# Column halves in the even steps, side sums one by one, and a round's next weights on VectorE: a change to a three-level fast matrix product in fp32

## The chip, the core and the metric

The kernel runs on one core of one Trainium2 chip. A core has a matrix engine (TensorE, PE in the profile; its weight loads are shown as PEld), three engines for elementwise work (VectorE or DVE, ScalarE or ACT, GpSimd or POOL) and SyncE (SP), whose queue here only issues transfers between the chip's main memory and the core's on-chip memory (SBUF). PE writes its results to eight accumulator banks (PSUM), each 128 partitions by 512 fp32 columns. Each engine works through its own list of instructions in order; an instruction that waits holds back everything behind it on its engine.

The metric is the device time of one launch in microseconds (us). Lower is better.

## What is computed

`x` has 32 batches of 128 channels by 2048 positions, all fp32. Cut to what matters here:

```
def reference(x, cond, ...):
    # a 128x128 mixing matrix per batch, made from cond by a small network and a softmax
    y = einsum('boi,bih->boh', agg_w, x) + agg_b
    # a 2048x2048 matrix W plus 16 low-rank updates, applied along the positions
    x = x + einsum('bsd,od->bso', y, W) + bias + low_rank(y)
    # a grouped convolution of 9 taps, then a blockwise MLP over permuted channels
    z = conv(x) + ctx + b
    return x + unpermute(down(gelu(up(permute(z)))))
```

The kernel multiplies `x` by the updated `W` first (the mixing matrix acts on the other axis and follows later). That product, 4096 rows by 2048 by 2048, is what the change is about.

## The kernel before

**The product.** It is a Strassen-Winograd scheme in three levels. At each level a 2x2 block product is made of seven products P1 to P7 of sums of blocks instead of eight.

- *Outer level:* seven rounds, in the order `P1, P2, P6, P7, P5, P3, P4` (`ROUNDS`). A round uses one sum of blocks of `W` as weights, and runs eight steps, `g` = 0 to 7, one for each group of four batches (512 columns of `x` transposed). `x_loads` fetches the blocks of `x` for a step, `x_combine` makes their sum `a` (in place, by `pieces`, line 282) and its four inner sums `s` (lines 310 to 313), all on GpSimd. Partial results (`p`, `u`, `c`) are fetched for a step by `part_load`, added to, and stored by `part_store`.
- *Inner level:* the round's weights need four sums per 128-row chunk: `inner_weights` makes `t1`, `t2`, `t4` (lines 251 to 253) and a difference in place (line 255). These are 16 GpSimd instructions of 128x512 for each round. They are issued in step 7 of the round ahead (in step 6 for the second round). The raw weights of the next round come from main memory through `outer_weights`, in steps 2 to 6.
- *Third level:* the rounds in `THIRD` (P2, P6, P7, P5, P3) take their steps in pairs. A step makes some of the seven inner products whole, each of four 128x512 matmuls: P1, P6, P7 in the four "wide" rounds, and P1, P5, P6, P3, P7 in round P5. The others (P2 and P4, in wide rounds also P3 and P5) are made for both steps of the pair together, in the odd step, again by seven products each: `quarter(w, k, ...)`, four matmuls of 128x256 that fill one bank (line 495). Their weight sums are made by `third_weights` in step 0: by GpSimd in `apart` (line 398), and by VectorE from a list `quarter_ops`, two at a time at the `between(j)` points of step 0 (line 1177), eight in a wide round, four in round P5. Their sums of `x` are made on VectorE by `first_inputs` (at the end of the even step) and `second_inputs` (in the odd step, behind the first addition): four instructions each in `third_inputs`, lines 431 to 434.

**The order around the change** is written out by hand. In `multiply_third` a product is four matmuls into a bank `px` (line 479), and VectorE adds the bank to the result in SBUF at once (`add`, line 469; `add_two` for P7, line 473). The next product goes on accumulating in the same bank, so its first matmul waits until VectorE has read the bank:

```
        product("P1", px, True, False)
        add(0, 0, px)
        ...
        product("P6", px, False, False)
        add(0, 1, px)
```

In an even step nothing stands between the two; in an odd step quarters do, in other banks. The quarters' results are added by lines 505 and 508.

**Between rounds P1 and P2** a side chain (`small()`, a generator that is advanced once or twice a step) makes the mixing matrices: `mixed_kernels` multiplies, copies each bank with ScalarE into one of three small buffers (line 610), and sends it out by four transfers of 32x512 from ScalarE's own queue (line 614). ScalarE also copies banks to the results in round P1 (line 344).

**Buffers.** Nearly everything lies in 24 rotating buffers of 128x2048 (`slot`); a new tile waits until the one that had its buffer has been read for the last time. SP's queue issues all loads and result stores in program order.

Of the kernel before, what the change touches and what calls it, by code (L numbers as in the profile page):

```python
# [11 lines left out]
ALU = mybir.AluOpType  # L12
# [4 lines left out]
P = 128  # L17
B = 32
# [37 lines left out]
def adaln_ffn_kernel(  # L56
# [184 lines left out]
        for ki in range(2):  # L241
            nc.vector.tensor_tensor(wsum[:, oh], wsum[:, oh], t[:, ki], ALU.add)

    def inner_weights(name, ts, between=lambda kc: None):

        t1, t2, t4 = (slot(f"{name}_t{k}", (P, 4, QW)) for k in (1, 2, 4))
        tt = nc.gpsimd.tensor_tensor
        for kc, t in enumerate(ts):
            between(kc)
            b11, b12, b21, b22 = (t[:, ki, oi] for ki in range(2) for oi in range(2))  # L250
            tt(t1[:, kc], b12, b11, ALU.subtract)
            tt(t2[:, kc], b22, t1[:, kc], ALU.subtract)
            tt(t4[:, kc], b21, t2[:, kc], ALU.subtract)
        for t in ts:
            tt(t[:, 0, 1], t[:, 1, 1], t[:, 0, 1], ALU.subtract)
        return {
            "t4": t4,
            "P1": [t[:, 0, 0] for t in ts], "P2": [t[:, 1, 0] for t in ts],
            "P3": [t[:, 1, 1] for t in ts], "P7": [t[:, 0, 1] for t in ts],
            "t1": t1, "P4": [t4[:, kc] for kc in range(4)], "P5": [t1[:, kc] for kc in range(4)],  # L260
            "P6": [t2[:, kc] for kc in range(4)],
        }
# [32 lines left out]
    def x_combine(r, g, ts):  # L295

        a = ts[0]
        tt = nc.gpsimd.tensor_tensor
# [8 lines left out]
        xa[steps.index((r, g))] = a  # L307
        s = slot(f"s_{r}{g}", (P, 4, QW))
        a11, a12, a21, a22 = a[:, 0, 0], a[:, 1, 0], a[:, 0, 1], a[:, 1, 1]
        tt(s[:, 1], a21, a22, ALU.add)  # L310
        tt(s[:, 2], s[:, 1], a11, ALU.subtract)
        tt(s[:, 3], a11, a21, ALU.subtract)
        tt(s[:, 0], a12, s[:, 2], ALU.subtract)
        xs_[steps.index((r, g))] = s
# [5 lines left out]
    xa, xs_ = {}, {}  # L320


    ADDED = {
        "P1": [(None, "p1")],
# [55 lines left out]
    def third_weights(name, rhs):  # L380
# [12 lines left out]
        def apart(k, t):  # L393

            for kc in range(2):
                (r11, r12), (r21, r22) = (halves(rhs[k][2 * h + kc]) for h in range(2))
                for op in sums(r11, r12, r21, r22, [v and v[:, kc] for v in t]):
                    nc.gpsimd.tensor_tensor(*op, ALU.subtract)

        def together(n, t):  # L400
            (r11, r12), (r21, r22) = (
# [25 lines left out]
    def third_inputs(x, t):  # L427

        (x11, x12), (x21, x22) = x
        tt = nc.vector.tensor_tensor  # L430
        tt(t[0], x21, x22, ALU.add)
        tt(t[1], t[0], x11, ALU.subtract)
        tt(t[3], x12, t[1], ALU.subtract)
        tt(x21, x11, x21, ALU.subtract)
        return {
            "P1": x11, "P2": x12, "P3": t[3], "P4": x22,
            "P5": t[0], "P6": t[1], "P7": x21,
        }
# [7 lines left out]
    def first_inputs(i):  # L446

        a, b = xa[i], xa[i + 1]
        return third_inputs(
            [blocks_of(t[:, 1]) for t in (a, b)],  # L450
            [as_two(a[:, 0, 1]), as_two(b[:, 0, 1]), None, as_two(a[:, 0, 0])],
        )

    def second_inputs(i):
        a, b = xs_[i], xs_[i + 1]
        return third_inputs(
            [blocks_of(t[:, 0:2]) for t in (a, b)],
            [as_two(a[:, 2]), as_two(a[:, 3]), None, as_two(xa[i + 1][:, 0, 0])],
        )

    def multiply_third(i, r, g, lhs, olds, between, rhs, quarters, sq):
# [2 lines left out]
        py = None if wide else bank()  # L464
        both = [held.pop(), olds] if sq else []

        def add(si, oi, ps):
            for acc in olds:
                nc.vector.tensor_tensor(acc[:, si, oi], ps, acc[:, si, oi], ALU.add)  # L469

        def add_two(ps):
            for acc in olds:
                nc.vector.tensor_tensor(
                    acc[:, 1], ps.unsqueeze(1).to_broadcast([P, 2, QW]), acc[:, 1], ALU.add
                )

        def product(k, ps, first, last):
            for kc in range(4):
                nc.tensor.matmul(  # L479
                    ps, lhsT=lhs[k][:, bass.ts(kc, P)], rhs=rhs[k][kc],  # L480
                    start=first and kc == 0, stop=last and kc == 3, skip_group_check=True,
                )

        qs = [{n: bank() for n in "xyz"} for w in quarters if sq and w is not None]
        xq = [sq]
# [1 line left out]
        def quarter(w, k, *to):  # L487
# [24 lines left out]
        product("P1", px, True, False)  # L512
        add(0, 0, px)
        if sq and wide:
            xq.append(second_inputs(i - 1))
        between(0)
        for w in range(2 if sq else 0):
            quarter(w, "P1", (0, 0))
            quarter(w, "P2", (0, 0))
        if not wide:  # L520
            product("P5", py, True, False)
            add(1, 1, py)
        between(1)
        if not wide and sq:
            quarter(0, "P6", (0, 1))
            quarter(0, "P5", (1, 1))
        product("P6", px, False, False)
        add(0, 1, px)
        between(2)
        if wide:  # L530
            for w in range(2 if sq else 0):
                quarter(w, "P6", (0, 1))
                quarter(w, "P5", (1, 1))
        elif sq:
            quarter(0, "P7", (1, 1))
            quarter(0, "P3", (0, 1))
        if not wide:
            product("P3", py, False, True)
            add(0, 1, py)
            done(py)  # L540
            between(3)
            if sq:
                quarter(0, "P4", (1, 0))
        product("P7", px, False, True)
        add_two(px)
        done(px)
        if wide:
            between(3)
            for k, to in (("P7", (1, 1)), ("P3", (0, 1)), ("P4", (1, 0))):
                for w in range(2 if sq else 0):  # L550
                    quarter(w, k, to)
        between(4)
        between(5)
        if not sq:
            held.append(olds)
            return
        for b, accs in enumerate(both):
            for (_, new), acc in zip(ADDED[r], accs):
                part_store(new, g - 1 + b, acc, nc.sync)
# [35 lines left out]
    def mixed_kernels(j, bd):  # L595

        w = mix.rearrange("p i o -> p (i o)")
        rows_of = [slice(h * P // 2, (h + 1) * P // 2) for h in range(2)]
        for n in range(2):
            cols = slice(n * QW, (n + 1) * QW)  # L600
            ps = [bank() for h in range(2)]
            for h in range(2):
                m = 2 * h + j
                nc.tensor.matmul(
                    ps[h], lhsT=bd[rows_of[h], m * P : (m + 1) * P], rhs=w[rows_of[h], cols],
                    start=True, stop=True,
                )
            for h in range(2):
                t = conv_tile(0, 4 * j + 2 * n + h, ("cq", "cs", "cr")[(2 * n + h) % 3])
                nc.scalar.copy(t, ps[h])  # L610
                done(ps[h])
                for q in range(4):
                    o0 = (4 * (2 * h + j) + q) * 2 * QW + n * QW
                    nc.scalar.dma_start(ag_d[:, o0 : o0 + QW], t[q * B : (q + 1) * B])

    def mix_loads(b):
        g, tp, s = b // GB, b % GB // 2, b % 2
# [306 lines left out]
    def small():  # L924
# [80 lines left out]
            nc.vector.tensor_scalar(orow[:, g], pos, g * L, None, ALU.add)  # L1005
        yield
        for j in range(2):
            mixed_kernels(j, bd)
            yield

        while len(made) < 16:
            yield
# [104 lines left out]
    for i, (r, g) in enumerate(steps):  # L1117
        ri = i // NG
        last_round = ri + 1 == len(ROUNDS)
        if i + 1 < len(steps):  # L1120
            if i + 1 not in xs:
                xs[i + 1] = x_loads(*steps[i + 1])
            if not last_round:
                lhs[i + 1] = x_combine(*steps[i + 1], xs.pop(i + 1))
                if r in THIRD and g == 0:
                    quarters, quarter_ops = third_weights(r, rhs)
        if i == 0:
            olds_load(0)
        if i + 1 < len(steps) and not last_round:
# [2 lines left out]
        if ahead and steps[i + 2][0] != "P6":  # L1132
            xs[i + 2] = x_loads(*steps[i + 2])
        if g == NG - (1 if ri else 2) and ri < len(ROUNDS) - 1:
            nxt = inner_weights(ROUNDS[ri + 1], [nxt[kc] for kc in range(4)])

        if ri == 0:
            ks = blocks[4 + 2 * g : 6 + 2 * g]
# [20 lines left out]
                waiting[g - 2] = outer_weights(ROUNDS[ri + 1], g - 2)  # L1159

        if last_round and g == 0:
            late_loads()
        if last_round and g == 2:

# [6 lines left out]
        def between(j):  # L1171
            if ri == 0 and j == 2:
                for k in blocks[6 + 2 * g : 8 + 2 * g]:
                    wt[k] = w_load(*k)
            for _ in range(2):
                if r in THIRD and j < 4 and quarter_ops:
                    nc.vector.tensor_tensor(*quarter_ops.pop(0), ALU.subtract)
# [124 lines left out]
```

## Time and profile before

| | |
|---|---|
| Time, median of 3 runs | 2681.66 us (2679.14 to 2686.1) |
| The profiled execution | 2681.12 us, its span 2679.4 us |
| PE busy | 2581.2 us, 96% of the span |
| DVE, POOL, ACT busy | 1544.7 us (58%), 1336.3 us (50%), 537.5 us (20%) |
| Granted PE clock | 0.99 over the span |
| Matmul, 128x512 at line 479 | 1088 records, two for each matmul |
| Result additions, lines 469 and 505, 128x512 from a bank | 683 to 689 ns |
| POOL at line 282 (`pieces`) | 1390 ns mean, 128 of `xt<-xt,xt` |

How to read it: one fp32 matmul leaves two PE records. PE records overlap (the mean of one 128x512 record is 592 ns or more, but one starts every 429 ns when nothing is waited for), so what a matmul costs is read from the distance between starts. "Idle before" is the time in which the engine had nothing to run before the instruction, with the instruction of another engine that ended the wait. A tile name such as `P_t` stands for all of a kind, here the inner sums `t1`, `t2`, `t4`; `wo_P` are raw weights of a round, `P_q` quarters' weight sums, `p` and `u` partial results.

### The profile page before, as it was taken

To read this page: it belongs to the slowest core of one execution; us is meant where nothing else is said; L and a number is where in the kernel's file an instruction comes from. 1 tells how busy PE (TensorE), PEld (TensorE's weight loads), DVE (VectorE), ACT (ScalarE), POOL (GpSimd) and SP (SyncE) were. 2 spreads that over 40 slices of the span, in tenths; PEclk is the share of its full clock that TensorE was granted. 3 is DMA by queue.
4 is the path that set the end of the run, shared out by engine and by line. 5 is a ranking of instruction groups with operands and counts; after the bars stand their busy time and mean duration, and the time that the engine had idled before them with its cause. 6 is when DMAs were issued, how large, how long until landed. Compare 5 with 4: busy or idle time off the path is not lost. (4 is left out here: it accounts for less than half of the span.)

```text
span 2679.4 us, 22365 instructions
## 1 busy us (share of the span) xinstructions
PE 2581.2 (96%) x7350; PEld 1394.7 (52%) x7350; DVE 1544.7 (58%) x2326; ACT 537.5 (20%) x1107; POOL 1336.3 (50%) x1086
## 2 busy tenths in 40 slices
PE   9999799989889999999999999999999999999998
PEld 4444366656556655466544555445555445555543
DVE  4554166655466566665446766666666666666600
ACT  0000100000000000000001234444444444444432
POOL 7221466897786674687423324444333444443322
PEclk9999899999999999999999999999999999999999
DMA  7542357758646476755567688777877777877532
GB/s 313 204 173 110 96 229 257 301 218 323 229 187 283 189 284 267 301 218 216 200 223 247 223 289 278 246 227 245 253 239 224 226 229 241 250 231 232 164 132 86
DMA packets 185091, 608.40 MB, mean 227 GB/s; under 512 B 17680, under 2 KB 88848, under 8 KB 140944
## 3 DMA queue, kind: packets, MB, share of 16 engines
q1 hardware_dynamic: 149936, 473.74, 49.9%
q0 software_dynamic: 32704, 130.04, 14.4%
q10 hardware_dynamic: 2336, 3.19, 0.4%
q8 instruction: 59, 0.97, 0.1%
q14 instruction: 56, 0.46, 0.1%
HBM read 372.51 MB, written 200.84 MB: 214 GB/s over the span
## 5 line engine op out<-in xcount | busy, mean ns | idle before, releaser
L884 PE MATMUL bank<-t,ws 128*128 128x512 f32 x1024 | 460.3, 592 | 0.0
L895 PE MATMUL bank<-gl,ws 128*128 128x512 f32 x1024 | 460.2, 592 | 0.0
L902 POOL DMA_INDIRECT out<-t,orow x128 | 152.9, 1194 | 540.9 <-DVE t L900 462.9
L887 ACT ACTIVATE gl<-bank 128x512 f32<-128x512 f32 x512 | 306.2, 598 | 445.3 <-PE bank L884 441.6
L895 PEld LDWEIGHTS bank<-gl,ws 128*128 128x128 f32 x1024 | 194.6, 190 | 233.0 <-issue 230.8
L884 PEld LDWEIGHTS bank<-t,ws 128*128 128x128 f32 x1024 | 194.6, 190 | 226.6 <-issue 222.9
L633 POOL TENSOR_TENSOR x<-x,fb 128x512 f32<-128x512 f32 x128 | 176.4, 1407 | 219.5 <-DMA x<-in_x 189.3
L900 DVE TENSOR_TENSOR t<-bank,t 128x512 f32<-128x512 f32 x128 | 88.4, 691 | 319.2 <-PE bank L895 319.2
L639 ACT ACTIVATE bank<-w,aggb 128x512 f32<-128x512 f32 x128 | 80.8, 683 | 899.6 <-DMA w<-w_d 882.1
L282 POOL TENSOR_TENSOR xt<-xt,xt 128x512 f32<-128x512 f32 x128 | 173.5, 1390 | 120.6 <-DMA xt<-in_xT 67.0
L310 POOL TENSOR_TENSOR s_P<-xt 128x512 f32<-128x512 f32 x56 | 75.1, 1341 | 295.9 <-DMA xt<-in_xT 218.6
L479 PE MATMUL bank<-P_t,s_P 128*128 128x512 f32 x384 | 178.1, 609 | 33.0 <-DVE p L469 24.3
L479 PE MATMUL bank<-wo_P,s_P 128*128 128x512 f32 x320 | 149.4, 613 | 18.9 <-DVE u L469 13.2
L868 POOL DMA_INDIRECT t<-hx_d,row x128 | 131.4, 1026 | 50.4 <-issue 25.3
L505 DVE TENSOR_TENSOR u<-bank,u 128x512 f32<-128x512 f32 x168 | 111.6, 687 | 63.4 <-PE bank L495 61.7
L479 PEld LDWEIGHTS bank<-P_t,s_P 128*128 128x128 f32 x384 | 73.0, 194 | 123.7 <-issue 103.8
L349 PE MATMUL bank<-P_t,s_P 128*128 128x512 f32 x256 | 115.3, 604 | 13.3 <-ACT m_P L344 13.3
L740 PE MATMUL bank<-va,tw_l 128*128 128x256 f32 x512 | 121.6, 380 | 0.4 <-DVE va L724 0.4
L495 PE MATMUL bank<-P_q,xt 128*128 128x256 f32 x480 | 112.9, 386 | 8.6 <-DVE u L505 4.6
L740 PEld LDWEIGHTS bank<-va,tw_l 128*128 128x128 f32 x512 | 96.9, 190 | 42.0 <-issue 32.2
L651 DVE TENSOR_TENSOR x<-bank,x 128x512 f32<-128x512 f32 x128 | 87.7, 690 | 49.3 <-POOL x L633 23.9
L648 PE MATMUL bank<-u,agl 128*128 128x512 f32 x256 | 115.1, 592 | 0.0
(207 smaller groups left out, 3971.4 us busy)
## 6 DMA issues: line engine op xcount, KB each, us to landing
xt<-in_xT SPq DMA_DIRECT2D x88, 1024.0 KB, 10.0
u<-u_d SPq DMA_DIRECT2D x40, 1024.0 KB, 10.0
wo_P<-wb_d SPq DMA_DIRECT2D x36, 1024.0 KB, 12.0
u<-c_d SPq DMA_DIRECT2D x64, 512.0 KB, 7.2
x<-in_x SPq DMA_DIRECT2D x32, 1024.0 KB, 7.9
xg<-x SPq DMA_DIRECT2D x256, 128.0 KB, 5.4
hx_d<-x1t SPq DMA_DIRECT2D x32, 1024.0 KB, 6.0
hx_d<-ht SPq DMA_DIRECT2D x32, 1024.0 KB, 7.0
```

Of the source, the lines that this page charges most:

```text
L282: nc.gpsimd.tensor_tensor(out[:, i, j], a[:, i, j], b[:, i, j], op)
L349: nc.tensor.matmul(ps, lhsT=lhs[k][:, bass.ts(kc, P)], rhs=rhs[k][kc], start=first and kc == 0, stop=last and kc == 3, skip_group_check=True,)
L479: nc.tensor.matmul(ps, lhsT=lhs[k][:, bass.ts(kc, P)], rhs=rhs[k][kc], start=first and kc == 0, stop=last and kc == 3, skip_group_check=True,)
L495: nc.tensor.matmul(out, lhsT=xq[w][k][:, i, bass.ts(kc, P)], rhs=quarters[w][i][k][kc], start=k in ("P1", "P2", "P5") and i == 0 and kc == ...
L633: nc.gpsimd.tensor_tensor(xt[:, f], xt[:, f], late["fb"][:, f], ALU.add)
L648: nc.tensor.matmul(pm, lhsT=ag, rhs=u[:, f], start=False, stop=True, skip_group_check=True)
L740: nc.tensor.matmul(out, lhsT=w[:, 2 * i + r], rhs=rhs, start=first and r == 0, stop=last and r == 1, skip_group_check=True,)
L868: nc.gpsimd.indirect_dma_start(out=t.rearrange("p k t -> p (k t)"), out_offset=None, in_=hx_d[g].rearrange("l k t -> l (k t)"), in_offset= ...
L884: nc.tensor.matmul(pu, lhsT=w[:, m * P : (m + 1) * P], rhs=t[:, 0], start=True, stop=True)
L887: nc.scalar.activation(gl[m], pu, AF.Gelu)
L895: nc.tensor.matmul(pd, lhsT=w[:, (MC + m) * P : (MC + m + 1) * P], rhs=gl[m], start=(m == 0), stop=(m == MC - 1),)
L902: nc.gpsimd.indirect_dma_start(out=out, out_offset=bass.IndirectOffsetOnAxis(ap=orow[:, g, h : h + 1], axis=0), in_=t[:, 1], in_offset=None,)
```

## The change

It has five parts.

1. *Column halves.* In wide rounds the whole products of the even steps, and of steps 1 and 7, are split in two column halves (`parts`): four matmuls of 128x256 on the left half of the bank, its addition, then the right half and its addition.
2. *Side sums one by one.* VectorE's other work of these rounds goes into a list `side`, and `fill` issues from it: one instruction behind each addition (`many` = 1; 2 in steps 0 and 7) and behind each quarter. The list takes the quarters' weight sums, `second_inputs`, and the fourth of `first_inputs`; the first three of these stay at the end of the even step. Two scratch tiles (`cx`, and the second half of `mix`) take the place of parts of `x` that were overwritten.
3. *Inner weights on VectorE.* For all rounds from P6 on, `t1`, `t2` and the difference (12 instructions) go from GpSimd to VectorE, in step 7 of the round ahead; `t4` (four) goes to VectorE at step 0 of the round itself (for the last round it stays on GpSimd).
4. *Order in steps 1 and 7.* In step 7 all quarters are made first and the whole products after them; in step 1 the whole products first and all quarters after them. In round P6 the inner sums `s` of odd steps go from GpSimd to VectorE (`held_back`, before `first_inputs`), and the in-place differences of `apart` are issued one step later (`overwriting`).
5. *Mixing matrices.* ScalarE copies the banks to one 128x2x1024 tile per call (`mk`), and eight transfers of 32x1024 go out from SP's queue two advances later (`mixed_store`).

```diff
+    def fill(n=1):
+        for _ in range(min(n, len(side))):
+            side.pop(0)()
...
-            tt(t4[:, kc], b21, t2[:, kc], ALU.subtract)
+            (put_last if tt == put_inner else tt)(
+                t4[:, kc], b21, t2[:, kc], ALU.subtract
+            )
...
+            if r == "P6" and g % 2:
+                held_back.append(op)
+            else:
+                nc.gpsimd.tensor_tensor(*op)
...
-            [as_two(a[:, 0, 1]), as_two(b[:, 0, 1]), None, as_two(a[:, 0, 0])],
+            [as_two(a[:, 0, 1]), as_two(conv_tile(i, "", "cx")), None, as_two(a[:, 0, 0])],
...
+        mixed = sq and g not in (1, NG - 1)
+        parts = [slice(0, QW)] if mixed or not wide else [slice(h * NQ, (h + 1) * NQ) for h in range(2)]
+        many = 1 if 0 < g < NG - 1 else 2
+
+        def product(k, ps, first, last, si=None, oi=None):
+            for cols in parts:
+                for kc in range(4):
+                    nc.tensor.matmul(
+                        ps[:, cols], lhsT=lhs[k][:, bass.ts(kc, P)], rhs=rhs[k][kc][:, cols],
+                        start=first and kc == 0 and cols == parts[0],
+                        stop=last and kc == 3 and cols == parts[-1], skip_group_check=True,
+                    )
+                for acc in olds:
+                    ...
+                    nc.vector.tensor_tensor(to, ps_, to, ALU.add)
+                fill(many)
...
+        if sq and g == NG - 1:
+            for n in range(4):
+                quarters_of(n)
+            side.extend(lambda op=op: nc.vector.tensor_tensor(*op) for op in inner)
+            inner.clear()
+        for n, full in enumerate(fulls):
+            full()
+            between(n)
+            if mixed and n < 4:
+                quarters_of(n)
...
+        if sq and g == 1:
+            for n in range(4):
+                quarters_of(n)
...
+        if g == NG - 1:
+            fill(len(side))
         for b, accs in enumerate(both):
             for (_, new), acc in zip(ADDED[r], accs):
                 part_store(new, g - 1 + b, acc, nc.sync)
...
+        t = slot(f"mk_{j}", (P, 2, 2 * QW))
...
-                t = conv_tile(0, 4 * j + 2 * n + h, ("cq", "cs", "cr")[(2 * n + h) % 3])
-                nc.scalar.copy(t, ps[h])
+                nc.scalar.copy(t[:, h, cols], ps[h])
...
-                for q in range(4):
-                    o0 = (4 * (2 * h + j) + q) * 2 * QW + n * QW
-                    nc.scalar.dma_start(ag_d[:, o0 : o0 + QW], t[q * B : (q + 1) * B])
+    def mixed_store(j, t):
+        for h in range(2):
+            for q in range(4):
+                o0 = (4 * (2 * h + j) + q) * 2 * QW
+                nc.sync.dma_start(ag_d[:, o0 : o0 + 2 * QW], t[q * B : (q + 1) * B, h])
...
-            mixed_kernels(j, bd)
+            mk = mixed_kernels(j, bd)
             yield
+            yield
+            mixed_store(j, mk)
...
                     quarters, quarter_ops = third_weights(r, rhs)
+                    for op in last + [(*op, ALU.subtract) for op in quarter_ops]:
+                        later(*op)
+                    last.clear()
+                if r in THIRD and g == 1:
+                    for op in overwriting:
+                        nc.gpsimd.tensor_tensor(*op, ALU.subtract)
+                    overwriting.clear()
...
-            nxt = inner_weights(ROUNDS[ri + 1], [nxt[kc] for kc in range(4)])
+            nxt = inner_weights(
+                ROUNDS[ri + 1], [nxt[kc] for kc in range(4)],
+                tt=put_inner if ri else nc.gpsimd.tensor_tensor,
+            )
...
         if in_pair(r, g) and g % 2 == 0:
-            sq = first_inputs(i)
+            for op in held_back:
+                nc.vector.tensor_tensor(*op)
+            held_back.clear()
+            first_ops, sq = first_inputs(i)
+            for op in first_ops[:3]:
+                nc.vector.tensor_tensor(*op)
+            del first_ops[:3]
```

More of the change, by code (lines that the diff above doesn't have):

```diff
@@ L242, in row_sums, with put_inner, put_last, later @@
             nc.vector.tensor_tensor(wsum[:, oh], wsum[:, oh], t[:, ki], ALU.add)
-    def inner_weights(name, ts, between=lambda kc: None):
+    xa, xs_ = {}, {}
+    side, held_back, inner, last, overwriting = [], [], [], [], []
+    def put_inner(*op):
+        inner.append(op)
+    def put_last(*op):
+        last.append(op)
+    def later(*op):
+        side.append(lambda: nc.vector.tensor_tensor(*op))
+    def fill(n=1):
+        for _ in range(min(n, len(side))):
+            side.pop(0)()
+    def inner_weights(name, ts, between=lambda kc: None, tt=nc.gpsimd.tensor_tensor):
         t1, t2, t4 = (slot(f"{name}_t{k}", (P, 4, QW)) for k in (1, 2, 4))
-        tt = nc.gpsimd.tensor_tensor
         for kc, t in enumerate(ts):
@@ L297, in x_combine @@
         a = ts[0]
-        tt = nc.gpsimd.tensor_tensor
         if r == "P6":
@@ L306, in x_combine @@
             pieces(a, a, ts[1], ALU.add if r == "P5" else ALU.subtract)
-        xa[steps.index((r, g))] = a
+        i = steps.index((r, g))
+        xa[i] = a
         s = slot(f"s_{r}{g}", (P, 4, QW))
         a11, a12, a21, a22 = a[:, 0, 0], a[:, 1, 0], a[:, 0, 1], a[:, 1, 1]
[L310 to L314, printed above, removed]
+        for op in (
+            (s[:, 1], a21, a22, ALU.add), (s[:, 2], s[:, 1], a11, ALU.subtract),
+            (s[:, 3], a11, a21, ALU.subtract), (s[:, 0], a12, s[:, 2], ALU.subtract),
+        ):
+            if r == "P6" and g % 2:
+                held_back.append(op)
+            else:
+                nc.gpsimd.tensor_tensor(*op)
+        xs_[i] = s
         return {
@@ L318, in x_combine @@
         }
-    xa, xs_ = {}, {}
     ADDED = {
@@ L396, in apart @@
                 (r11, r12), (r21, r22) = (halves(rhs[k][2 * h + kc]) for h in range(2))
-                for op in sums(r11, r12, r21, r22, [v and v[:, kc] for v in t]):
+                ops = sums(r11, r12, r21, r22, [v and v[:, kc] for v in t])
+                for op in ops[:3]:
                     nc.gpsimd.tensor_tensor(*op, ALU.subtract)
+                overwriting.append(ops[3])
         def together(n, t):
@@ L429, in third_inputs @@
         (x11, x12), (x21, x22) = x
[L430 to L435, printed above, removed]
+        ops = [
+            (t[0], x21, x22, ALU.add), (t[1], t[0], x11, ALU.subtract),
+            (t[3], x12, t[1], ALU.subtract), (x21, x11, x21, ALU.subtract),
+        ]
+        return ops, {
             "P1": x11, "P2": x12, "P3": t[3], "P4": x22,
@@ L457, in second_inputs @@
             [blocks_of(t[:, 0:2]) for t in (a, b)],
-            [as_two(a[:, 2]), as_two(a[:, 3]), None, as_two(xa[i + 1][:, 0, 0])],
+            [as_two(t) for t in (a[:, 2], a[:, 3])]
+            + [None, mix[:, 4:8].rearrange("p (s k) o -> p s (k o)", s=2)],
         )
@@ L465, in multiply_third @@
         both = [held.pop(), olds] if sq else []
[L467 to L482, printed above, removed]
+        mixed = sq and g not in (1, NG - 1)
[10 more added lines that the diff above has]
+                for acc in olds:
+                    if si is None:
+                        to = acc[:, 1, :, cols]
+                        ps_ = ps[:, cols].unsqueeze(1).to_broadcast([P, 2, cols.stop - cols.start])
+                    else:
+                        to, ps_ = acc[:, si, oi, cols], ps[:, cols]
+                    nc.vector.tensor_tensor(to, ps_, to, ALU.add)
+                fill(many)
         qs = [{n: bank() for n in "xyz"} for w in quarters if sq and w is not None]
@@ L510, in quarter @@
                 done(ps)
-        product("P1", px, True, False)
-        add(0, 0, px)
+            fill()
         if sq and wide:
[L515 to L519, printed above, removed]
-        if not wide:
[L521 to L550, printed above, removed]
-                    quarter(w, k, to)
-        between(4)
-        between(5)
+            ops, x = second_inputs(i - 1)
+            xq.append(x)
+            side[0:0] = [
+                lambda op=op: nc.vector.tensor_tensor(*op)
+                for op in (ops[0], ops[1], first_ops.pop(), ops[2], ops[3])
+            ]
+        elif sq:
+            later(*first_ops.pop())
@@ new lines, in multiply_third @@
+        fulls = [
+            lambda: product("P1", px, True, False, 0, 0), lambda: product("P6", px, False, False, 0, 1),
+            lambda: product("P7", px, False, True),
+        ]
+        if not wide:
+            fulls.insert(1, lambda: product("P5", py, True, False, 1, 1))
+            fulls.insert(3, lambda: product("P3", py, False, True, 0, 1))
+        groups = [
+            [("P1", (0, 0)), ("P2", (0, 0))], [("P6", (0, 1)), ("P5", (1, 1))],
+            [("P7", (1, 1)), ("P3", (0, 1))], [("P4", (1, 0))],
+        ]
@@ new lines, in quarters_of @@
+        def quarters_of(n):
+            for w in range(len(qs)):
+                for k, to in groups[n]:
+                    quarter(w, k, to)
+        if sq and g == NG - 1:
[8 more added lines that the diff above has]
+                quarters_of(n)
@@ L554, in multiply_third @@
+        done(*([px] if wide else [px, py]))
+        for j in range(len(fulls), 6):
+            between(j)
+        if mixed and wide:
+            quarters_of(3)
+        if sq and g == 1:
+            for n in range(4):
+                quarters_of(n)
         if not sq:
@@ L608, in mixed_kernels @@
             for h in range(2):
-                t = conv_tile(0, 4 * j + 2 * n + h, ("cq", "cs", "cr")[(2 * n + h) % 3])
-                nc.scalar.copy(t, ps[h])
+                nc.scalar.copy(t[:, h, cols], ps[h])
                 done(ps[h])
-                for q in range(4):
-                    o0 = (4 * (2 * h + j) + q) * 2 * QW + n * QW
-                    nc.scalar.dma_start(ag_d[:, o0 : o0 + QW], t[q * B : (q + 1) * B])
+        return t
+    def mixed_store(j, t):
[3 more added lines that the diff above has]
+                nc.sync.dma_start(ag_d[:, o0 : o0 + 2 * QW], t[q * B : (q + 1) * B, h])
     def mix_loads(b):
@@ L1161, in adaln_ffn_kernel @@
         if last_round and g == 0:
+            for op in last:
+                nc.gpsimd.tensor_tensor(*op)
             late_loads()
@@ L1174, in between @@
                     wt[k] = w_load(*k)
-            for _ in range(2):
-                if r in THIRD and j < 4 and quarter_ops:
-                    nc.vector.tensor_tensor(*quarter_ops.pop(0), ALU.subtract)
             if j == 3 and ahead and steps[i + 2][0] == "P6":
```

## The prediction, made before the changed kernel ran

> **What bounds the kernel now.** I read the page first: is there an engine whose idle time is the time to win?
>
> ```profile
> span 2679.4 us, 22365 instructions
> PE 2581.2 (96%) x7350; PEld 1394.7 (52%) x7350; DVE 1544.7 (58%) x2326; ACT 537.5 (20%) x1107; POOL 1336.3 (50%) x1086
> ```
>
> It is PE, with 98 us of idle time. The waits of PE say who ends it:
>
> ```profile
> PE bank L479 <- DVE p L469: 33.5, 17, 8.5
> PE bank L479 <- DVE u L469: 21.0, 19, 4.1
> PE bank L349 <- ACT m_P L344: 13.3, 1, 13.3
> PE bank L349 <- ACT cr L610: 3.3, 1, 3.3
> ```
>
> All four kinds are touched by the change. Then the busy time by rounds P2, P6, P7, P5, P3:
>
> ```profile
> core 0: us, PE busy (x) PEld busy (x) DVE busy (x) ACT busy (x) POOL busy (x), PEclk, DMA share, GB/s
> 329.60:525.54 195.94, 183.49 (x642) 121.86 (x641) 127.20 (x159) 3.00 (x5) 130.38 (x104) 0.99 0.67 257
> 525.54:739.45 213.91, 188.06 (x642) 123.00 (x641) 112.85 (x148) 0.00 (x0) 175.61 (x146) 0.95 0.68 260
> 739.45:935.99 196.54, 183.97 (x641) 121.10 (x640) 123.41 (x148) 0.00 (x0) 144.61 (x112) 0.99 0.55 219
> 935.99:1124.70 188.71, 186.69 (x545) 103.03 (x544) 117.69 (x156) 0.00 (x0) 111.61 (x89) 1.00 0.71 281
> 1124.70:1321.36 196.66, 183.71 (x641) 121.20 (x640) 121.22 (x148) 0.00 (x0) 145.33 (x114) 0.99 0.52 206
> ```
>
> Against these I set what PE needs without a wait. In undisturbed stretches of the timeline eight 128x512 records (four matmuls) start 3.43 us apart, four 128x256 records 0.863 us apart. A wide pair has 24 whole matmuls (20.6 us) and 14 quarters of 1.725 us (24.2): 44.8, a wide round 179.1. Round P5 needs 40 whole matmuls and 7 quarters a pair: 46.4, or 185.7 in all. So 16.8, 34.8, 17.4, 3.0 and 17.6 us are lost: 89.6. The fifth loss lies ahead of them, in the timeline:
>
> ```profile
> 306.40 0.59 ACT L610 COPY cq<-bank 128x512 f32<-128x512 f32 x1 [1.82 <-DMA ag_d<-cr]
> 307.01 1.74 ACTq L614 DMA_DIRECT2D ag_d<-cq  x4
> 308.85 0.59 ACT L344 COPY m_P<-bank 128x512 f32<-128x512 f32 x1 [1.87 <-DMA ag_d<-cq]
> 309.58 8.59 PE L349 MATMUL bank<-P_t,s_P 128*128 128x512 f32 x13 [13.34 <-ACT m_P L344]
> ```
>
> ScalarE's copy for PE stands behind its own transfers. The 13 records then take 8.59 us instead of 12 x 0.429 + 0.59 = 5.74: PE runs slow after a long idle time, 2.85 us more. With the 3.3 of L610 that is 19.5 us. All that the change can reach: 109 us.
>
> **Part by part.** *Mixing matrices.* Eight copies of 0.59 us without a transfer between them, in ScalarE's idle time; the 19.5 us go. The 16 new transfers stand in SP's queue; the first eight, at 0.33 us an issue, stand ahead of the `xt` load of round P2's step 1, which was issued at 330.83 and released GpSimd at 338.77. I take 3 us later for it and charge it below.
>
> *Halves in steps 2, 4, 6.* Each wide even step waits twice, 1.1 us a time (1.04 plus 0.07 in the starts): 12 steps x 2.2 = 26.6 us. Now the left half is added (0.42 us, row of L508, 128x256) while the right half runs (1.72 us). The waits go; without that cover each would be about 0.8 (0.42 and the way from PE and back). Splitting 288 matmuls costs 576 x (2 x 0.2157 - 0.429) = 1.4 us. The short waits of quarters for L505 (0.5 to 0.8 us, ten of them) go with the interleaving; the one at 406 (2.9 and a slow restart) hangs on GpSimd too, and I keep half, 2.4.
>
> *The borders of rounds.* Here VectorE gets work. What does one of its SBUF-only additions cost? The timeline shows three prices: GpSimd idle, GpSimd on 256 columns, GpSimd on 512.
>
> ```profile
> 1097.92 0.68 DVE L431 TENSOR_TENSOR xt<-xt 128x512 f32<-128x512 f32 x1
> ```
> ```profile
> 1150.08 1.10 DVE L433 TENSOR_TENSOR xt<-xt,xt 128x512 f32<-128x512 f32 x1
> 1150.70 2.19 POOL L398 TENSOR_TENSOR P_q<-wo_P,P_q 128x256 f32<-128x256 f32 x2
> ```
> ```profile
> 529.78 1.22 DVE L1177 TENSOR_TENSOR P_q<-P_t 128x512 f32<-128x512 f32 x1
> 531.10 3.24 DVE L1177 TENSOR_TENSOR P_q<-P_t,P_q 128x512 f32<-128x512 f32 x2
> 533.75 12.07 POOL L282 TENSOR_TENSOR xt<-xt,xt 128x512 f32<-128x512 f32 x8
> 535.93 0.68 DVE L469 TENSOR_TENSOR p<-bank,p 128x512 f32<-128x512 f32 x1
> 536.75 5.37 PE L479 MATMUL bank<-wo_P,s_P 128*128 128x512 f32 x8 [3.07 <-DVE p L469]
> 541.96 3.60 PE L479 MATMUL bank<-wo_P,xt 128*128 128x512 f32 x8
> ```
>
> 0.69, 1.1 and about 1.6 us; an addition from a bank keeps 0.68 beside GpSimd. The last two rows show the price of a slow restart after 3 us of idling: 5.37 against 3.60, 1.8 us. GpSimd is busy 707.5 of the five rounds' 991.8 us; the change takes about 76 inner and 16 held-back instructions at 1.3 from it, so some 588 of 960 stay, 61%. Price m of a moved instruction: 0.69 + 0.61 x (1.35 - 0.69) = 1.1, bounds 0.69 and 1.6.
>
> Now a chain of VectorE, from the start of step 7's whole products to the first addition of step 1 in the next round; each matmul there waits for an addition somewhere in it. Border P6 to P7: the first half 1.72; 12 half additions (8 x 0.42, 4 x 0.69) 6.1; 12 inner instructions, 4 `t4`, 8 quarter sums and 3 of `first_inputs`, 27m; one addition 0.42. PE needs 10.3 + 10.3 + 3.44 = 24.1 to the same point. 8.3 + 27m - 24.1 = 13.9, in two or three long waits (P6 of step 0, P6 of step 1), so two restarts: 17.5 us. The others the same way:
> - P2 to P6: four held-back instructions more, 18.3 + 3.6 = 21.9. Step 7 of round P6: its first quarters need no VectorE for 6.9 us, but held-back and input sums take 0.9 + 7m + 0.7 = 9.3: 2.4.
> - P7 to P5: after 12 inner ones P6 waits 2.2, and by step 1 it is 1.7 + 3.1 + 23m + 9.4 - 34.4 = 5.1 in all (additions here go to two results).
> - P5 to P3: 3.4 + 8.0 + 3.1 + 0.4 + 27m - 30.9 = 13.7, + 3.6 = 17.3.
> - P3 to P4: 1.7 + 3.1 + 12m + 0.7 - 17.2 = 1.5.
> - P1 to P2: no inner weights, but `xt` lands at about 12 us of step 0, then 3m, and then eight reductions for the chain of the convolution weights, 5.6 us, which ran ahead of step 0 before (326.97 to 332.4) and are now queued between `first_inputs` and step 1's additions: 12 + 3.3 + 5.6 + 0.4 - 13.8 = 7.6, + 1.8 = 9.4.
>
> Behind these additions stand PE's matmuls and, at the end of step 7, SP's stores and the loads queued behind them.
>
> Sum of what stays or is new: 17.5 + 21.9 + 2.4 + 5.1 + 17.3 + 1.5 + 9.4 + 2.4 + 1.4 = 79. So 109 - 79 = 30 us less than the profiled execution's 2681.1 (0.5 below the median): 2651, given as 2650. The slope is about 13 us for 0.1 in m: m = 0.69 leaves 26 (2598), m = 1.6 gives 144 (2716), and nothing is won at m = 1.33.
>
> A rule speaks against moving work this way. The Trainium skill's page "SBUF — State Buffer", section "Who interferes with whom", says that a VectorE instruction with two SBUF inputs and a GpSimd instruction that reads SBUF shut each other out until one is done. The rows agree that there is a price, but 1.6 is less than 0.69 + 1.27 for a whole GpSimd instruction; by the rule m would be 1.46 and the sum 2698.
>
> **Rivals.** (1) *The forecast*, m from 0.95 to 1.3: 2632 to 2677; chance 0.48. (2) *The burst finds GpSimd idle.* Its loads are queued behind step 7's stores, so it may have nothing to do in step 0; against it, `apart` and `pieces` can start as soon as buffers are free. m near 0.75 gives 2605; 0.19. (3) *VectorE becomes the bound at four borders, slower.* GpSimd, freed of 16 instructions, runs ahead into just these steps, both engines slow each other, m = 1.5: 2703. Place: steps 7 to 1 of rounds P2 to P3; it decides from m = 1.33, and rows of 1.62 and 1.75 in today's step 0 speak for it; 0.24. (4) *The mixing gain comes back*: the 16 transfers hold up SP's loads, so that PE waits 20 us in round P2 or its weights come late: 2670; 0.09.
>
> **How the numbers follow.** A measurement of this kernel tells about 0.3%, 8 us, from no change: 2673.6 to 2689.7. Rival 1 lies below for 0.43 and within for 0.05; 2 below; 3 above for 0.22, within for 0.02; 4 below 0.03, within 0.05, above 0.01. Faster 0.65, same 0.12, slower 0.23. The range, 2612 to 2698, takes in the forecast's own (2632 to 2677), most of rival 2 and the near end of rival 3.
>
> **What would show it.** Right: no idle time before L349 near 309; wide pairs of steps 2 to 5 at 44.8 to 45.5 us instead of 47.0; what PE idles, it idles in steps 0 and 1, ended by VectorE's half additions, with VectorE near 100% busy there and its moved instructions near 1.1 us. Wrong: a mean of these under 0.9 or over 1.35; waits of PE in step 7's quarters over 5 us; or a wait for a load or GpSimd as the longest of PE.

## The result, and the profile after

The changed kernel takes 2748.05 us in the median of four runs (2745.87 to 2750.01); the kernel before takes 2682.29 us beside it. The ratio is 1.0244, with a 95% interval from 1.0227 to 1.0262. The change makes the kernel 66 us slower; about 30 us faster, 2650, was forecast. Two pages of its profile answer to those shown of before. First the head of the page, and then PE's waits (engine, line waited for, total us, number, longest):

```profile
span 2744.1 us, 23538 instructions
PE 2601.2 (95%) x7926; PEld 1499.8 (55%) x7926; DVE 1601.7 (58%) x2490; ACT 536.7 (20%) x1107; POOL 1230.7 (45%) x994
```
```profile
PE bank L494 <- DVE p L505: 61.4, 59, 13.3
PE bank L494 <- DVE u L505: 58.8, 61, 7.5
PE bank L519 <- DVE u L529: 2.7, 3, 2.2
```

The two long kinds of before, 33.5 and 21.0 us in 17 and 19 waits, are now 61.4 and 58.8 us in 59 and 61 waits. Line 494 is the matmul of a whole product and line 505 its addition. ScalarE's two waits (13.3 and 3.3 us) are gone. The busy time by rounds P2, P6, P7, P5, P3, in the columns of before:

```profile
310.51:527.78 217.27, 189.13 (x786) 147.67 (x785) 124.44 (x191) 3.75 (x7) 119.16 (x97) 0.98 0.65 243
527.78:755.32 227.54, 191.02 (x786) 148.70 (x784) 144.28 (x199) 0.00 (x0) 162.51 (x132) 0.96 0.63 245
755.32:970.34 215.02, 189.03 (x786) 147.56 (x785) 130.20 (x183) 0.00 (x0) 122.74 (x91) 0.98 0.51 200
970.34:1160.78 190.44, 186.68 (x545) 102.92 (x544) 123.27 (x168) 0.00 (x0) 84.92 (x66) 1.00 0.70 276
1160.78:1385.30 224.52, 192.81 (x786) 149.92 (x785) 135.97 (x187) 0.00 (x0) 119.66 (x90) 0.95 0.46 183
```

Round P2 begins at 310.51 where it began at 329.60: the stall ahead of it is gone, 19.1 us won. Then each wide round takes 215 to 228 us where PE needs 179.1, and P5 190.4 where it needs 185.7. By the reckoning of the prediction the five rounds lose 172.6 us; before they lost 89.6. Where? The timeline of an even step far from any border, step 2 of round P6 (PE's weight loads and the other queues are left out; in brackets the idle time and what ended it):

```profile
599.00 1.89 PE L494 MATMUL bank<-wo_P,xt 128*128 128x256 f32 x8
...
600.93 0.42 DVE L505 TENSOR_TENSOR p<-bank,p 128x256 f32<-128x256 f32 x1 [0.58 <-PE bank L494]
...
601.41 1.99 PE L494 MATMUL bank<-wo_P,xt 128*128 128x256 f32 x8 [0.52 <-DVE p L505]
603.44 0.42 DVE L505 TENSOR_TENSOR p<-bank,p 128x256 f32<-128x256 f32 x1 [2.09 <-PE bank L494]
...
603.92 1.99 PE L494 MATMUL bank<-P_t,s_P 128*128 128x256 f32 x8 [0.52 <-DVE p L505]
605.95 0.42 DVE L505 TENSOR_TENSOR p<-bank,p 128x256 f32<-128x256 f32 x1 [2.09 <-PE bank L494]
```

The first eight records are the left half of P1, the next eight its right half. The right half doesn't run beside the left half's addition. It waits for it, and so does each half after it. The step takes 14.55 us (599.00 to 613.55), where 48 records of 128x256 need 10.36: 4.19 lost, against 2.2 in a step of before. Each half costs an addition of 0.42 us and the way from PE to VectorE and back. There are 24 steps with such halves, six in each of four wide rounds (0, 1, 2, 4, 6, 7). At this step's 4.19 us each they come to 101 of the 172.6 us; that is a reckoning, since in steps 7, 0 and 1 the halves stand among other waits. The other 72 us come on top there, at the borders of rounds.

### The profile page after: what moved, and what is told of

It is laid out like the page before. It is cut to its first block, busy times and chain, and to the rows that moved or that the text cites. A ratio compares the mean times of both kernels' runs of the same rounds, so it can differ in the third digit from the quotient of the medians.

```text
span 2744.1 us, 23538 instructions
## 1 busy us (share of the span) xinstructions
PE 2601.2 (95%) x7926; PEld 1499.8 (55%) x7926; DVE 1601.7 (58%) x2490; ACT 536.7 (20%) x1107; POOL 1230.7 (45%) x994
## 5 line engine op out<-in xcount | busy, mean ns | idle before, releaser
L334 POOL TENSOR_TENSOR s_P<-xt 128x512 f32<-128x512 f32 x104 | 146.0, 1403 | 298.2 <-DMA xt<-in_xT 180.5
L494 PE MATMUL bank<-P_t,s_P 128*128 128x256 f32 (+1 forms) x576 | 182.7, 462 | 29.6 <-DVE u L505 15.4
L505 DVE TENSOR_TENSOR u<-bank,u 128x512 f32<-128x512 f32 (+2 forms) x164 | 107.1, 673 | 161.9 <-PE bank L494 161.9
L494 PE MATMUL bank<-wo_P,s_P 128*128 128x256 f32 (+1 forms) x464 | 149.6, 467 | 25.2 <-DVE u L505 17.1
L494 PE MATMUL bank<-wo_P,xt 128*128 128x256 f32 (+1 forms) x400 | 127.4, 464 | 44.4 <-DVE u L505 26.2
L494 PEld LDWEIGHTS bank<-P_t,s_P 128*128 128x128 f32 x576 | 106.6, 192 | 99.3 <-issue 49.0
L901 POOL DMA_INDIRECT t<-hx_d,row x128 | 131.2, 1025 | 51.7 <-issue 25.6
L494 PEld LDWEIGHTS bank<-wo_P,s_P 128*128 128x128 f32 x464 | 85.2, 190 | 82.8 <-issue 44.7
L494 PEld LDWEIGHTS bank<-wo_P,xt 128*128 128x128 f32 x400 | 78.8, 201 | 83.1 <-DVE u L505 31.0
```

Of the source, the lines that this page charges most:

```text
L334: nc.gpsimd.tensor_tensor(*op)
L494: nc.tensor.matmul(ps[:, cols], lhsT=lhs[k][:, bass.ts(kc, P)], rhs=rhs[k][kc][:, cols], start=first and kc == 0 and cols == parts[0], sto ...
L505: nc.vector.tensor_tensor(to, ps_, to, ALU.add)
L901: nc.gpsimd.indirect_dma_start(out=t.rearrange("p k t -> p (k t)"), out_offset=None, in_=hx_d[g].rearrange("l k t -> l (k t)"), in_offset= ...
```

## The experiments

All ran beside the kernel before, whose median was 2680 to 2683 us. Where the five rounds' loss is given, it is worked out as in the prediction: the length from the first matmul of round P2 to the first of P4 in the timeline, less 902.1 us.

| Run | Median, us | Ratio, 95% interval |
|---|---|---|
| the change | 2748.05 | 1.0244 (1.0227 to 1.0262) |
| e1: two banks | 2660.09 | 0.9913 (0.9895 to 0.9931) |
| e2: no halves | 2715.93 | 1.0121 (1.0102 to 1.0140) |
| e3: before, part 5 alone | 2674.89 | 0.9973 (0.9963 to 0.9983) |
| e4: e3, even steps in two banks | 2655.21 | 0.9892 (0.9874 to 0.9910) |
| e12: e3, even steps in one bank | 2701.00 | 1.0069 (1.0052 to 1.0085) |
| e5: e1, inner weights on GpSimd | 2650.38 | 0.9883 (0.9866 to 0.9899) |
| e6: e1, old order of steps 1 and 7, these unsplit | 2650.76 | 0.9888 (0.9872 to 0.9905) |
| e7: e1, nothing held back | 2647.19 | 0.9870 (0.9854 to 0.9887) |
| e8: e1, `first_inputs` behind step 1's additions | 2634.10 | 0.9822 (0.9806 to 0.9839) |
| e9: e8 and e7 | 2625.06 | 0.9786 (0.9768 to 0.9804) |
| e10: e9 and e5 | 2644.29 | 0.9859 (0.9842 to 0.9876) |
| e11: e9, the convolution chain in two portions | 2629.80 | 0.9805 (0.9788 to 0.9822) |

### e1: is it the bank?

```diff
+        px = [bank() for _ in parts]
...
-            for cols in parts:
+            for cols, pb in zip(parts, ps):
                 for kc in range(4):
                     nc.tensor.matmul(
-                        ps[:, cols], lhsT=lhs[k][:, bass.ts(kc, P)], rhs=rhs[k][kc][:, cols],
-                        start=first and kc == 0 and cols == parts[0],
-                        stop=last and kc == 3 and cols == parts[-1], skip_group_check=True,
+                        pb[:, cols], lhsT=lhs[k][:, bass.ts(kc, P)], rhs=rhs[k][kc][:, cols],
+                        start=first and kc == 0, stop=last and kc == 3, skip_group_check=True,
```

> The changed kernel, but the left and the right column half of a whole product go to two different accumulator banks (wide rounds, steps 0, 1, 2, 4, 6, 7); all else is kept. Theory A (the right half waits for the left half's addition only because both lie in one bank): the 24 such steps lose 4.2 to 5.4 us each by their six serial additions, about 104 us; with two banks each keeps under 0.5 us, and what is left are the waits at the borders of rounds: 2748 - 104 + 5 = 2650, from 2640 to 2665. Rival B (VectorE's burst at the borders is the bound there, and the serial additions of steps 7, 0 and 1 only cover it): only the 12 steps 2, 4 and 6 gain 4.2 each, 2697. Rival C (PE's halves are held up by something else than the bank): 2748.

2660.09 us: theory A, 88 us less than the change by this one edit. The same kind of step in its timeline:

```profile
574.75 0.59 PE L494 MATMUL bank<-wo_P,xt 128*128 128x256 f32 x2
...
575.18 3.62 PE L494 MATMUL bank<-P_t,s_P 128*128 128x256 f32 x16
575.39 0.42 DVE L504 TENSOR_TENSOR p<-bank,p 128x256 f32<-128x256 f32 x1 [1.30 <-PE bank L494]
577.11 0.42 DVE L504 TENSOR_TENSOR p<-bank,p 128x256 f32<-128x256 f32 x1 [1.30 <-PE bank L494]
...
578.64 3.62 PE L494 MATMUL bank<-wo_P,s_P 128*128 128x256 f32 x16
```

The 16 records of P6 follow one another without a wait, and VectorE adds one half while PE fills the other. The step takes 10.36 us. The five rounds lose 84.4 us instead of 172.6. That this is 88 and not 101 is what rival B is right in: steps 2, 4 and 6 give 53 of it, steps 7, 0 and 1 the other 35, and there some 12 us of the serial halves had covered work of VectorE.

### e2: without halves

`parts = [slice(0, QW)]` in every step.

> The changed kernel with whole products everywhere (no column halves); all else is kept. Theory A: a whole step then waits twice for an addition of 0.69 us instead of five times for one of 0.42 and once of 0.69: 2.2 us lost instead of 4.25, in 24 steps 49 us, and 1.4 us of extra matmul starts: 2748 - 50 = 2698, from 2688 to 2708. Theory that the loss lies in VectorE's additional work and not in the halves: within 5 us of 2748.

2715.93 us, 18 above theory A's 2698. Even steps that wait for nothing else lose 2.1 to 2.2 us, as theory A has it. But `fill` issues once for each addition, so with three additions instead of six the list of side work empties half as fast, and more of it is left ahead of the next step's first addition. That would account for the rest: step 1 of rounds P2, P6, P7 and P3 now loses 14.4, 17.6, 11.0 and 10.7 us (10.1, 15.9, 4.3 and 6.1 in e1), step 0 of P6 and P7 14.3 and 7.9 (7.6 and 1.9). The edit changed two things; only the first was expected, and no run separates them.

### e4 and e12: halves alone, in two banks and in one

Both take the kernel before with part 5 (e3, below) and split the whole products of the wide rounds' even steps. They differ in one line, and in the start and stop flags and the release of the banks that go with it:

```diff
-        px = [bank() for _ in parts]
+        px = [bank()] * len(parts)
```

> The kernel before with part 5, and in wide rounds the whole products of even steps in column halves that lie in two banks; no other part of the change. Theory: the 12 steps 2, 4 and 6 lose 2.2 us each by waits, which go (26 us), and those of step 0 partly (0 to 8 us); the extra starts cost 1 us: 26 to 33 us less than the run with part 5 alone, so 2629 to 2637 if that one is at 2662. Rival (the time comes back as waits for loads or GpSimd in the odd steps): 10 us or less below the run with part 5 alone.

> As e4_mix_even_two (the kernel before with part 5 and column halves in the even steps of wide rounds, 2655), but with both halves in one bank, as the change has them; no other part of the change. Theory (the shared bank makes the six additions of a step serial, in the old order as in the new): an even step loses 4.2 us instead of 2.2 in the kernel with part 5 alone (2675), 16 steps: 2675 + 33 = 2708, from 2695 to 2712. Rival (the waits come from the changed kernel's other work on VectorE, not from the bank): 2655 to 2675.

2655.21 us with two banks, 2701.00 with one, 2674.89 with whole products. Thus the halves are worth 20 us in two banks, somewhat less than theory, and cost 26 us in one bank, in the old order and with none of the change's other parts. PE's waits for additions in the two:

```profile
PE bank L472 <- DVE p L482: 25.5, 8, 7.8
PE bank L472 <- DVE u L482: 9.8, 4, 4.8
```
```profile
PE bank L472 <- DVE p L483: 44.5, 41, 7.4
PE bank L472 <- DVE u L483: 33.3, 41, 4.5
```

Twelve waits against 82. Nearly all of steps 2, 4 and 6 fall to 10.36 us with two banks (12.53 before) and rise to 14.7 with one. Part of the gain comes back in e4 as longer odd steps, step 5 of rounds P2 and P6 (41.7 and 40.8 us instead of 36.1 and 34.5 in e3).

### e3: part 5 alone

> The kernel before with part 5 alone: ScalarE copies the mixing matrices to one tile a call, the transfers go out from SP's queue two advances later. The theory of the prediction: the stall of 19.5 us between 292 and 315 us goes: 2662, from 2658 to 2666. Rival: the 16 transfers in SP's queue hold up the loads of round P2 and the time is got back there: 2675 to 2682.

2674.89 us, 7.5 below the kernel before where theory said 19.5; the rival's lower end is 2675. Both are half right. Round P2 begins at 308.43, 21 us earlier. But the five rounds now lose 101.8 us instead of 89.6. Step 0 of round P6 alone goes from 6.1 to 15.2:

```profile
512.56 1.13 PE L479 MATMUL bank<-P_t,s_P 128*128 128x512 f32 x2 [0.51 <-POOL P_t L252]
...
516.46 1.12 PE L479 MATMUL bank<-P_t,s_P 128*128 128x512 f32 x2 [2.77 <-POOL P_t L252]
...
517.78 3.40 DVE L1183 TENSOR_TENSOR P_q<-P_t,P_q 128x512 f32<-128x512 f32 x2 [6.39 <-POOL P_t L253]
...
523.60 5.74 PE L479 MATMUL bank<-wo_P,s_P 128*128 128x512 f32 x8 [6.01 <-DVE p L469]
```

PE is now ahead of GpSimd's inner weights (line 252), and the long wait of 6.01 us leads to them too: VectorE, whose addition ends it, had stood 6.39 us for line 253. The stall had given GpSimd the time that it lacks here. Another 5.8 us go in step 1 of round P2, which loses 6.6 where it lost 0.8:

```profile
329.96 0.70 DVE L1024 STREAM_TRANSPOSE wsq<-wsum 128x512 f32<-128x512 f32 x1
...
334.71 0.69 DVE L1025 TENSOR_REDUCE small<-wsq 128x16 f32<-128x512 f32 x1
...
335.31 0.68 DVE L469 TENSOR_TENSOR p<-bank,p 128x512 f32<-128x512 f32 x1
...
336.14 5.37 PE L479 MATMUL bank<-P_t,s_P 128*128 128x512 f32 x8 [4.57 <-DVE p L469]
```

There the eight instructions for the convolution weights (lines 1024 and 1025) have come to stand ahead of the addition, as the prediction's term for the border P1 to P2 has it. In neither place is it the transfers' place in SP's queue that takes the gain, as the rival had it, but an engine that is late once PE is early.

### e5, e6, e7: each of the other parts undone in e1

e5 issues the inner weights on GpSimd (`tt=nc.gpsimd.tensor_tensor`); e6 sets `mixed = sq` and drops the two blocks that put all quarters first in step 7 and last in step 1; e7 sends round P6's odd sums of `x` to GpSimd again.

> The kernel with two banks (2660), with the inner weights of all rounds back on GpSimd (part 3 undone); all else is kept. Theory A (VectorE's burst from step 7 to step 1 sets the end of the borders, as the prediction has it): VectorE has 16 instructions less at four borders, and its waits of PE there (about 8, 5, 2 and 11 us at the borders into P6, P7, P5 and P3) go for the most part: 2638 to 2648. Theory B (GpSimd is the later of the two at the borders): its 16 instructions of 1.3 us make its sums for step 1 late, and PE waits for it or for VectorE behind it: 2662 to 2680.

> The kernel with two banks (2660), with the quarters of steps 1 and 7 between the whole products, as in steps 3 and 5 (the order of part 4 undone). Theory A (the order of steps 1 and 7 is what shelters VectorE's burst): step 1's quarters wait for GpSimd's weight sums and the second whole product for the burst: 10 to 25 us slower, 2670 to 2685. Theory B (the order matters little, the burst has to be paid either way): within 6 us of 2660.

> The kernel with two banks (2660), with the four sums of x of round P6's odd steps back on GpSimd. Theory A (the two longest waits, 12.8 us at step 1 and 11.8 us in step 7 of round P6, stand behind these four instructions on VectorE): both shrink by 5 us or more, 2645 to 2652. Theory B (GpSimd is the one that is late in round P6): its sums come after 13.4 us of other additions, PE waits for GpSimd instead, 2660 to 2675.

2650.38, 2650.76 and 2647.19 us: each of these parts costs about 10 us while the others stand. In e5 both theories act: round P3's first two steps win 7 us and step 1 of P6 5, but step 0 of P6, where PE waits for GpSimd's weights, goes from 7.5 to 18.2 us.

In e6, where the whole products of these two steps aren't split either, neither theory fits the time. What the order does shows by steps: without it the wide rounds and P5 lose 13 us in steps 0 and 1 instead of 57, but 59 in step 7 instead of 25. Step 7 of round P5 alone loses 26.6 us:

```profile
1077.57 0.69 DVE L563 TENSOR_TENSOR P_t<-wo_P 128x512 f32<-128x512 f32 x1 [18.07 <-POOL xt L299]
1078.17 1.28 DVE L528 TENSOR_TENSOR u<-bank,u 128x512 f32<-128x512 f32 x2
1079.51 3.39 PE L518 MATMUL bank<-P_q,cx 128*128 128x256 f32 x8 [15.94 <-DVE u L528]
```

An inner weight (line 563) now stands in VectorE's list ahead of the quarters' additions and waits 18 us for GpSimd, and they wait behind it. So the order of part 4 shelters step 7 and puts the burst into steps 0 and 1; most of it is paid either way, as theory B says, and on balance the order costs more than it saves.

In e7 the median is theory A's; the wait of 12.6 us (12.8 in the expectation) becomes 5.0 and that of 11.6 in step 7 becomes 2.1 and 2.5. Its profiled execution, 2653.70 us, is the slowest of four (the others 2645.48 to 2648.37): there round P6 wins 11.7 us, and P7 and P3 give 8.5 of them back.

### e8: what stands ahead of step 1's first addition

The longest wait of the change (13.3 us) and of e1 (12.6) end at the same place. The end of step 0 of round P6, in the changed kernel:

```profile
548.24 13.39 POOL L299 TENSOR_TENSOR xt<-xt,xt 128x512 f32<-128x512 f32 x8
548.76 1.74 DVE L1250 TENSOR_TENSOR s_P<-xt 128x512 f32<-128x512 f32 x1
550.54 1.63 DVE L1250 TENSOR_TENSOR s_P<-s_P,xt 128x512 f32<-128x512 f32 x1
552.10 1.74 DVE L1250 TENSOR_TENSOR s_P<-xt 128x512 f32<-128x512 f32 x1
553.76 1.75 DVE L1250 TENSOR_TENSOR s_P<-xt,s_P 128x512 f32<-128x512 f32 x1
555.43 1.74 DVE L1254 TENSOR_TENSOR xt<-xt 128x512 f32<-128x512 f32 x1
557.21 1.63 DVE L1254 TENSOR_TENSOR cx<-xt 128x512 f32<-128x512 f32 x1
558.88 1.63 DVE L1254 TENSOR_TENSOR xt<-xt,cx 128x512 f32<-128x512 f32 x1
560.44 0.41 DVE L505 TENSOR_TENSOR p<-bank,p 128x256 f32<-128x256 f32 x1
560.77 1.41 DVE L541 TENSOR_TENSOR s_P<-s_P 128x512 f32<-128x512 f32 x1
560.90 2.50 PE L494 MATMUL bank<-wo_P,xt 128*128 128x256 f32 x5 [13.34 <-DVE p L505]
```

Seven instructions of VectorE stand one behind the other beside eight of GpSimd, and the addition that PE waits for is the eighth. The three of line 1254 (`first_inputs`) are wanted by the quarters alone, and in step 1 the quarters come last:

```diff
-            for op in first_ops[:3]:
-                nc.vector.tensor_tensor(*op)
-            del first_ops[:3]
+            if g:
+                for op in first_ops[:3]:
+                    nc.vector.tensor_tensor(*op)
+                del first_ops[:3]
...
-                for op in (ops[0], ops[1], first_ops.pop(), ops[2], ops[3])
+                for op in (*first_ops[:-1], ops[0], ops[1], first_ops.pop(), ops[2], ops[3])
```

> The kernel with two banks (2660), in which the three instructions of first_inputs that follow step 0 go behind the additions of step 1 one by one, since step 1's quarters come last and nothing needs them sooner. Theory A (step 1's wait is VectorE's queue: three instructions of 1.1 to 1.7 us stand ahead of the first addition): the waits at step 1 shrink by 3 to 5 us in each of four wide rounds, 2643 to 2650. Theory B (GpSimd or a load ends these waits): within 5 us of 2660.

2634.10 us, 26 below e1, more than theory A said. Step 1 of the five rounds loses 16.4 us in all, in e1 38.2 (10.1, 15.9, 4.3, 1.9, 6.1).

### e9, e10, e11: what is left

> The kernel with two banks and the three instructions of first_inputs behind step 1's additions (2634), with the four sums of x of round P6's odd steps back on GpSimd. Theory A (both edits shorten the same thing, VectorE's queue, and add up): the waits of 7.6 and 11.3 us in round P6 shrink by 8 to 12 us together, 2622 to 2627. Theory B (with the first edit GpSimd is already the later one in round P6): within 4 us of 2634.

> As the run before it, with the inner weights of all rounds on GpSimd too. Theory A (VectorE's burst still decides at the borders, the waits of 1.5, 1.5, 4.9 and 6.2 us there): 8 to 12 us below the run before it. Theory B (with first_inputs out of its way VectorE has room for the inner weights, and GpSimd is the later one): 3 to 10 us above it.

> As e9_spread_no_held, with the eight instructions of the convolution weights' chain on VectorE (4 x 0.70 and 4 x 0.69 us) issued in two portions, four at the end of step 0 of round P2 and four at the end of step 1. Theory: the wait of 3.3 us in step 1 of round P2, which stands behind all eight, loses up to 2.8 us: 2 to 4 us below e9_spread_no_held. Rival: GpSimd's late sums for that step end the wait: no change within 1.5 us.

e9: 2625.06 us, theory A; the two edits nearly add up (35 us below e1, alone 26 and 13). This is the fastest kernel, 2.1% below the one before; its five rounds lose 55.7 us. e10: 2644.29 us, theory B, and by more than it said. PE's waits in e10, the two longest kinds:

```profile
PE bank L518 <- POOL wo_P L1166: 17.8, 3, 9.9
PE bank L494 <- POOL P_t L267: 7.1, 3, 3.5
```

Both end with GpSimd. The inner weights on VectorE cost 10 us in e1 and are worth 19 us in e9. The two kernels differ in the place of `first_inputs` and in who makes round P6's odd sums, GpSimd again in e9 and e10; which of the two decides, no run shows. e11: 2629.80 us, 5 above e9, and neither expectation. The wait that it was to shorten (3.3 us in the expectation, 2.5 in e9) is gone, but the chain of the convolution weights is later, and waits of 2.2 us at 451 and of 4.2 at 521 (1.6 in e9) have appeared; how the one leads to the other stays open.

## Why the prediction was wrong

**The step that failed** is "Now the left half is added (0.42 us, row of L508, 128x256) while the right half runs (1.72 us). The waits go". They don't go, because both halves lie in one bank, and in this program a matmul waits for an addition that still reads its bank, though the two touch different columns. (Each bank is one tile of the program, so the runs don't tell whether the wait goes by the bank or by the tile.) The prediction had the price of a wait without cover, about 0.8 us, and that is what each half pays: in step 2 of round P6 halves start 2.51 us apart, where 1.73 are needed. The wait of the next product for its own half was reckoned with; the wait of the right half for the left half's addition was not. The term was 1.4 us of additional starts for 26.6 us of waits won. In the changed kernel it is 101 us in 24 steps; e1 against the change shows 88 us for the bank alone, e12 against e4 46 us in 16 steps without the other parts.

The rule was to be had. The Trainium skill's page "PSUM — Partial Sum Buffer", section "PSUM bank collisions raise a hardware error", says that TensorE writing a bank and VectorE reading it at the same time, on the same 32 partitions, is an error of the chip even where the columns are disjoint, and that PSUM has to be guarded by bank, not by address. This case agrees as far as it goes: in the steps shown, no half in one bank runs beside the other's addition, and in two banks each does. What the chip would do without the wait, no run shows.

**Mixing matrices.** "The 19.5 us go" was right: round P2 begins 19.1 us earlier in the change, 21 in e3. That it can be lost again in round P6 was not in the sum; rival 4 had it lost to SP's loads, and e3 shows 9 us of it at GpSimd's inner weights and 6 in step 1 of round P2, the latter a part of the term for P1 to P2.

**The borders.** Here the sum came out, in part by luck. The price m of a moved instruction was put at 1.1; the 172 that the changed kernel's timeline has between 300 and 1250 us took 1.08 us in the mean. The sum of what stays at the borders was 79 us; e1, which has the change's borders and halves that overlap, loses 84.4. The forecast's 2650 is thus nearly e1's 2660: with the bank's share taken out, 10 us are missing. From step 7's whole products to the end of step 1, e1 loses 27.4 us at P2 to P6 (forecast 21.9), 15.1 at P5 to P3 (17.3), 3.5 at P7 to P5 (5.1) and 10.9 at P1 to P2 (9.4). Two terms were far off and happened to make up for each other: P6 to P7, 17.5 forecast and 6.6 in e1, and step 7's quarters of round P6, 2.4 forecast and 13.5 in e1.

**The rivals.** Rival 3, the one on the slow side, named VectorE's burst with m = 1.5 as what would make the kernel slower. The sign came out as in rival 3 and its cause did not. None of the three signs named under "wrong" appeared in the change: the mean is 1.08, step 7's quarters of round P6 lose 4.6 us, and PE's longest wait ends with VectorE. All three concern the borders or the loads; the one that decided is the second under "right", "wide pairs of steps 2 to 5 at 44.8 to 45.5 us instead of 47.0". Step 2 and step 3 of round P6 take 49.0.

**What the change could have been.** With two banks it is 0.9% faster than before, and with `first_inputs` and the held-back sums moved as in e9, 2.1%. Part 5 and the even steps' halves in two banks alone (e4) are 1.1% faster: as e1 has them, parts 2 to 4 bring nothing beyond that.

## What to carry to other kernels

Splitting a product so that its addition runs beside the rest took two banks here; two halves of one bank make every half wait, and more pieces then mean more waits. Before an overlap is priced, look in the built program for the semaphore that the second piece waits on. An instruction's place in its engine's list can count more than the engine's load: three instructions that nobody needed yet, put ahead of the addition that PE waited for, cost 26 us. And what a move of work between engines is worth depends on the rest: the same move was worth -10 us in e1 and +19 in e9.

## What the runs showed of the hardware beside this

An addition of VectorE can last as long as a whole run of GpSimd's beside it, as if it were shut out. In step 7 of round P6 of e1:

```profile
680.91 5.60 DVE L1249 TENSOR_TENSOR s_P<-s_P,xt 128x512 f32<-128x512 f32 x1
681.04 4.92 POOL L299 TENSOR_TENSOR wo_P<-wo_P,wo_P 128x512 f32<-128x512 f32 x4
```

One instruction that takes 0.69 us alone lasts 5.60, while four of GpSimd's go by at 1.23 each; the changed kernel has one of 4.27 at 712.71 beside three. Elsewhere the two take turns: the eight of GpSimd at 548.24 last 1.67 us each, and VectorE's beside them 1.63 to 1.75. So the price of 1.7 us beside GpSimd isn't the worst case. That GpSimd is the reason is read from the rows; no run tests it, and what decides between taking turns and being shut out stays open.
